# A graph-attention stack whose instruction order is set by the kernel's own list scheduling

## The chip, the cores and the metric

The kernel runs on one core of a Trainium2 chip. A core has TensorE (PE; its weight loads are listed apart as PEld), VectorE (DVE), ScalarE (ACT), GpSimd (POOL) and SyncE (SP); SP and POOL start the transfers here. Each engine works through its own stream of instructions in the order in which they stand, and waits at an instruction until the semaphores that it names are reached. The metric is the device time of the whole kernel in microseconds (us), the median of several runs.

## The reference

The input is x, 32 batches of 512 nodes with 256 features, and one 512 x 512 adjacency matrix that all batches share. Four layers follow each other, each `x = x + layer(relu(layernorm(x)), adj)`:

- Layers 0 and 1 are single-head graph attentions: `Wh = h W`, a score `leaky_relu(s_i + s_j)` for each pair of nodes, where s_i and s_j are products of Wh with two vectors, a softmax over the neighbours, and the weighted mean of Wh, behind which stands an elu (layer 0) or a relu (layer 1).
- Layer 2 is the same with four heads of 64 features.
- Layer 3 is a small network: a linear layer to 512 with relu, an attention over all nodes without a mask (`_gat(relu(out), None, W_fc, a_fc)`), elu and a residual, a linear layer back to 256, a masked attention, elu, a residual and a relu.

All is float32.

## The kernel before

Nodes lie on the 128 partitions in four blocks. A batch's x is one tile of 128 x 4 x 256. Exponentials of scores factor, so that the weights of a pair are `max(r_i, t_j) * mask` and need no exponential of their own: `weights` (line 339) turns the column of r into a row on all partitions by four transposes into a PSUM bank, and DVE makes the four 128 x 512 blocks of w (L353). `aggregate` then multiplies them with the values v on TensorE, and a column of the product is the softmax's denominator, whose reciprocal (L387) scales the result on ACT.

`values` (line 308) makes v: two matmuls into a bank, an exponential of three columns on ACT (L319, L322), in layer 1 a small product on DVE (L324), and a scaled copy of the 256 features on ACT (L320, L325). Layer 2 does it with L462 on ACT and the product L463 on DVE, which reads the bank out. `norm` (L269 to L280) is the layernorm on DVE with two small steps on ACT; `turn_pair` transposes its result and ACT writes it as hT (L290).

The unmasked attention of layer 3 is computed by sorting in all batches but the last (`sort_attend`, line 556): `project_half` (L528, L529 on ACT) makes the values; DVE and ACT count ranks (L586, L599); POOL scatters rows to DRAM in sorted order (L607, eight transfers a batch); SP fetches them as `sums` (L614, L615); DVE builds running sums on each partition (L625 to L632), TensorE carries them over partitions with two matmuls against triangles (`before`, `after`), and DVE adds that (L641, L644); SP writes the result to a table in DRAM (L647, L648). Then POOL gathers one row for each node (L655, four transfers a batch, `g` with two buffers), DVE combines its two halves (L670), and ACT and DVE make elu(elu) of it (L387, L674, L675, L410, L411, L412). `mlp_in` transposes that and adds it to oT (L730).

Four streams (NS = 4) of batches run against each other, 75 model-us apart (LEAD). Each is a generator that yields the time at which it next wants to go on; a loop at the end of `fast` always resumes the stream that is due first. That sets the order in which the program is written down. Each stream has two PSUM banks of its own (8 banks in all) and takes those of idle streams too. The framework's own scheduler then places the instructions on the engines: among those that are ready by its model of durations, the one written first goes first. At five places the kernel ties an instruction to the written order (`keep_in_program_order`): at the minimum of adj (L215) and the first transpose of the mask, at layer 2's weights for j = 0, at the copy T (L625) and at L670.

Of the kernel before, what the change touches and what calls it, by code (L numbers as in the profile page):

```python
# [8 lines left out]

# [1 line left out]

# [11 lines left out]
OP = mybir.AluOpType  # L25
AX = mybir.AxisListType

EPS = 1.0e-5
P = 128
# [2 lines left out]
TINY = 1.0e-30  # L32
CYCLES = 2400.0

@with_exitstack
def fast(ctx, tc, flag, x, adj, w0, a0, w1, a1, w2, a2, mlp1_w, mlp1_b, mlp2_w, mlp2_b,
         w_fc, a_fc, w_hand, a_hand, out):
    nc = tc.nc
    B, N, F = x.shape
# [8 lines left out]
    SLOW = 1.5  # L48
    STRETCH = 2.0

    const = ctx.enter_context(tc.tile_pool(name="const", bufs=1))
    work = ctx.enter_context(tc.tile_pool(name="work", bufs=2))
    psum = ctx.enter_context(tc.tile_pool(name="psum", bufs=1, space=bass.MemoryType.PSUM))
    dram = ctx.enter_context(tc.tile_pool(name="dram", bufs=1, space=bass.MemoryType.DRAM))

    turn = [0]
    begun = [0.0]
# [7 lines left out]
        spent[0] += 4 * max(x.shape[-1], P)  # L65
        nc.tensor.matmul(p, w, x, **flags)  # L66

    def transpose(p, x, i, tied=False):
        spent[0] += 2 * P
        instruction = nc.tensor.transpose(p, x, i)  # L70
        if tied:
            tc.keep_in_program_order(instruction)

    active = set()
    banks = [0]
# [9 lines left out]
    ident = const.tile([P, P], FP, name="ident")  # L85
# [5 lines left out]
    seen = const.tile([P, 5 * B], FP, name="seen")  # L91
# [60 lines left out]
    W0, _ = fetched0 = fetch_w(w0, a0_sb, "W0")  # L152
    adj_sb = work.tile([P, NT, N], I32, tag="w", name="adj", bufs=4)
# [3 lines left out]
    W1, _ = fetched1 = fetch_w(w1, a1, "W1")  # L157
# [6 lines left out]
    for h in range(NH):  # L164
        t, r = divmod(h * D, P)
# [8 lines left out]
    WFC, _ = fetched3 = fetch_w(w_fc, a_fc, "WFC")  # L174
    WM2 = const.tile([P, KH, F], FP, name="WM2")
    nc.sync.dma_start(WM2, mlp2_w.rearrange("(k p) f -> p k f", p=P))
    WHA, _ = fetched4 = fetch_w(w_hand, a_hand, "WHA")
# [8 lines left out]
    C = F + 2  # L186
# [14 lines left out]
    differ = const.tile([P, 2], FP, name="differ")  # L201
# [5 lines left out]
    def setup():  # L207

        own = work.tile([P, NT, N], FP, tag="w", name="own", bufs=4)
        nc.vector.tensor_scalar(own, adj_sb, 0.0, None, op0=OP.is_gt)  # L210
        nc.gpsimd.affine_select(
            out=own, in_=own, pattern=[[P, NT], [-1, N]], base=0, channel_multiplier=1,
            compare_op=OP.not_equal, fill=1.0,
        )
        tc.keep_in_program_order(nc.vector.tensor_reduce(differ[:, 0:1], adj_sb, AX.XY, OP.min))  # L215
        nc.vector.tensor_scalar(differ[:, 0:1], differ[:, 0:1], 0.0, None, op0=OP.is_lt)
        for j in range(NT):
            turn[0] = NS - 1 - j % (NS - 1)
            p = bank()
            for t in range(NT):  # L220
                transpose(p[:, t * P:(t + 1) * P], own[:, t, j * P:(j + 1) * P], ident, j + t == 0)
            nc.scalar.copy(maskT[:, j, :], p)
        turn[0] = NS - 1
        yield
        yield from finish_w(fetched1, 0.01)


        least = small([1], "rden")
        nc.vector.tensor_reduce(least, diag, AX.X, OP.min)
        nc.vector.tensor_scalar(differ[:, 1:2], least, 0.0, None, op0=OP.is_le)  # L230
        nc.vector.tensor_copy(W2[:, :, :, :D], raw2.rearrange("p k (h d) -> p k h d", d=D))
        nc.vector.tensor_scalar_mul(A2v[:, :, 1:2], A2v[:, :, 0:1], -0.8)
        nc.vector.tensor_scalar_mul(A2v[:, :, 2:3], A2v[:, :, 2:3], 0.8)
        for k in range(KF):
            project(W2[:, k, :, D:], lambda k, f: raw2[:, k, f * P:(f + 1) * P], k, A2)
            yield
        yield from finish_w(fetched3, 0.2)

        for tri, sign in ((before, 1), (after, -1)):
            nc.vector.memset(tri, 1.0)  # L240
            nc.gpsimd.affine_select(
                out=tri, in_=tri, pattern=[[sign, P]], base=0, channel_multiplier=-sign,
                compare_op=OP.is_gt, fill=0.0,
            )
        ties = work.tile([P, 2 * N - P], FP, tag="w", name="ties", bufs=4)
        nc.vector.memset(ties, TINY)
        nc.gpsimd.affine_select(
            out=ties, in_=ties, pattern=[[-1, 2 * N - P]], base=N - P, channel_multiplier=1,
            compare_op=OP.is_gt, fill=0.0,
        )  # L250
        nc.vector.tensor_copy(band, ties)
        yield
        yield from finish_w(fetched4, 0.2)
# [89 lines left out]
    def weights(r_col, t_col, masked=True, r=None):  # L343

        landed = r is not None
        if not landed:
            r = bank()
            for t in range(NT):
                transpose(r[:, t * P:(t + 1) * P], r_col(t).to_broadcast([P, P]), ident)
        wt = work.tile([P, NT, N], FP, tag="w", name="w", bufs=4)  # L350
        for j in range(NT):
            if masked:
                w = nc.vector.scalar_tensor_tensor(  # L353
                    wt[:, j, :], r, t_col(j), maskT[:, j, :], op0=OP.max, op1=OP.mult
                )
                if landed and j == 0:
                    tc.keep_in_program_order(w)
            else:
                nc.vector.tensor_scalar(wt[:, j, :], r, t_col(j), None, op0=OP.max)
        return wt  # L360
# [202 lines left out]
    def sort_attend(oT, b):  # L563

        halves, ends = fc_values()
        orders = [dram.tile([N, C], FP, tag=f"order{c}", name=f"order{c}", bufs=2) for c in range(2)]
        at = work.tile([P, 2, NT], U32, tag="at", name="at", bufs=4)
        table = tables[b % 2]
# [9 lines left out]
        p = bank()  # L578
# [25 lines left out]
        for c in range(2):  # L604
# [7 lines left out]
            u = flat[c].rearrange("p (t k) n -> p t k n", k=2)[:, :, 1, :]  # L612
# [6 lines left out]
        for c in range(2):  # L619
            yield sort  # L620
            sums = flat[c].rearrange("p (t k) n -> p t k n", k=2)
            u = sums[:, :, 1, :]

            T = small([NT], "T")
            tc.keep_in_program_order(nc.vector.tensor_copy(T, u[:, :, F + 1]))  # L625
            tot = work.tile([P, C], FP, tag="tot", name="tot", bufs=1)
            nc.vector.tensor_tensor(sums[:, 2, 0, :], u[:, 0, :], u[:, 1, :], op=OP.add)
            nc.vector.tensor_tensor(sums[:, 3, 0, :], sums[:, 2, 0, :], u[:, 2, :], op=OP.add)
            nc.vector.tensor_tensor(tot, sums[:, 3, 0, :], u[:, 3, :], op=OP.add)
            nc.vector.tensor_scalar_mul(u[:, 3, :], u[:, 3, :], T[:, 3:4])  # L630
            for t in (2, 1, 0):
                nc.vector.scalar_tensor_tensor(  # L632
                    u[:, t, :], u[:, t, :], T[:, t:t + 1], u[:, t + 1, :], op0=OP.mult, op1=OP.add
                )
            yield after_us(3)

            pv, pu = bank(), bank()
            matmul(pv[:, :C], before, tot, start=True, stop=True)
            matmul(pu[:, :C], after, u[:, 0, :], start=True, stop=True)
            nc.scalar.copy(sums[:, 0, 0, :], pv[:, :C])  # L640
            nc.vector.tensor_tensor(  # L641
                sums[:, 1:, 0, :], sums[:, 1:, 0, :], pv[:, None, :C].to_broadcast([P, NT - 1, C]), op=OP.add
            )
            nc.vector.tensor_tensor(u, u, pu[:, None, :C].to_broadcast([P, NT, C]), op=OP.add)  # L644
            q = 3 * P // 4
            nc.vector.tensor_tensor(tot[q:, :], tot[q:, :], pv[q:, :C], op=OP.add)  # L646
            nc.sync.dma_start(places[:, :, c, :], flat[c])  # L647
            nc.sync.dma_start(table[N:, c * C:(c + 1) * C], tot[P - 1:, :])  # L648
            sort = after_us(1)
# [13 lines left out]
        landed = after_us(6)  # L663
        for t in range(NT):
            yield landed
            y, q = pair(), pair("q")
            g = gs[t]
            z = g[:, :2 * C]
            tc.keep_in_program_order(
                nc.vector.scalar_tensor_tensor(z, z, ends[:, t, 2:3], g[:, 2 * C:], op0=OP.mult, op1=OP.add)  # L670
            )
            rd = reciprocal(z[:, F:F + 1])
            z = z.rearrange("p (c n) -> p c n", c=2)[:, :, :F]
            nc.scalar.activation(q, z, AF.Exp, scale=rd)  # L674
            nc.scalar.activation(y, z, AF.Relu, scale=rd)  # L675
            elu2_plus1(y, q)
            if t + 2 < NT:
                gather(t + 2)
            got.append(y)
            landed = after_us(3)  # L680
            when.append(after_us(4))
            if t == 0:
                continue
            yield when[t - 1]
            mlp_in(oT, got[t - 1], t - 1)
# [84 lines left out]
    while ready:  # L770
        i = min(ready, key=ready.get)
# [23 lines left out]
    p = bank()  # L795
    transpose(p[:1, :P], bad, ident)
    one = const.tile([1, 1], FP, name="one")
    nc.vector.tensor_reduce(one, p[:1, :P], AX.X, OP.max)
    nc.vector.tensor_scalar(flag, one, 0.5, None, op0=OP.is_gt)


@with_exitstack
# [430 lines left out]
```

## Time and profile before

Three runs gave 2930.02, 2930.80 and 2934.68 us; the median is 2930.8 us. The profiled execution has a span of 2929.6 us from its first to its last instruction; the page gives no other time for it.

| engine | busy us | share of the span | instructions |
|---|---|---|---|
| PE (matmul) | 2858.9 | 98% | 15177 |
| PEld (weight loads) | 2329.5 | 80% | 15177 |
| DVE | 2219.9 | 76% | 5676 |
| ACT | 1536.8 | 52% | 3922 |
| POOL | 502.3 | 17% | 515 |

The DMA engines moved 270.89 MB, 92 GB/s over the span. A float32 matmul is recorded as two passes, a transpose as one, so the 15177 records are some 8850 instructions. "Busy" for PE adds up where any matmul is in flight; a matmul of 257 columns is recorded with 382 ns, while the next one starts 217 ns after it.

How to read what follows: in the order of time, a line has its start in us, its duration in us, the engine, the kernel's line, the operation, what it writes and reads, a shape and how many were merged; in brackets behind it how long the engine stood idle ahead of it and what released it.

### The profile page before, as it was taken

How to read it: one execution, taken by the hardware profiler on the slowest of the kernel's cores; microseconds unless marked ns; L12 is line 12 of the kernel's file. 1: busy time of each engine (PE TensorE's matmuls, PEld its weight loads, DVE VectorE, ACT ScalarE, POOL GpSimd, SP SyncE). 2: the span in 40 equal slices, each digit the busy share in tenths (PEclk: the TensorE clock that was granted, in tenths of full speed). 3: DMA queues.
4: the chain of work that ended last, by engine and by line, in shares of the span. 5: the costliest groups of instructions: out<-in, count | busy, mean ns of one | idle time of the engine just before them, and what ended most of it. 6: DMA issues, size and time to landing. Idle time of an engine off the chain costs nothing.

```text
span 2929.6 us, 43083 instructions
## 1 busy us (share of the span) xinstructions
PE 2858.9 (98%) x15177; PEld 2329.5 (80%) x15177; DVE 2219.9 (76%) x5676; ACT 1536.8 (52%) x3922; POOL 502.3 (17%) x515
## 2 busy tenths in 40 slices
PE   8999999999999999999999999999999999999998
PEld 6777887877888877888877888788887788877876
DVE  4677877778778778778778777787787787777764
ACT  4444455555555555555554556545555555555444
POOL 0011112112122111122021121111221111211220
PEclk9999999999999999999999999999999999999999
DMA  3033223233223333233332233222332322323230
GB/s 94 19 102 102 80 88 116 91 98 95 88 94 106 93 100 98 84 102 96 100 102 80 89 115 93 91 97 91 94 116 80 102 93 88 104 93 96 90 107 30
DMA packets 193182, 270.89 MB, mean 92 GB/s; under 512 B 17024, under 2 KB 156094, under 8 KB 192960
## 3 DMA queue, kind: packets, MB, share of 16 engines
q1 hardware_dynamic: 163200, 169.76, 18.5%
q0 software_dynamic: 29760, 98.30, 10.4%
q8 instruction: 123, 2.02, 0.3%
q14 instruction: 99, 0.81, 0.1%
HBM read 152.62 MB, written 115.39 MB: 91 GB/s over the span
## 4 chain that ended last, share of the span: by engine, by line
PE 82%; DVE 10%; ACT 4%; DMA 3%; issue 1%; SPq 0%; POOL 0%; DVEq 0%; POOLq 0%; ACTq 0%
PE b L66 75%; PE b L70 7%; DVE st L269 2%; DMA g<-table,at 2%; DVE sums L641 1%; DVE xn L280 1%; DVE x L406 1%; DVE y L405 1%; ACT v L325 1%; DVE sums L632 1%; ACT y L505 1%; ACT q L504 1%; DVE w L353 1%; ACT hT L290 1%; DVE tot L646 0%
## 5 line engine op out<-in xcount | busy, mean ns | idle before, releaser
L66 PE MATMUL b<-v,w 128*128 128x65 f32 (+1 forms) x7232 | 1218.0, 321 | 10.6 <-DVE w L353 10.5
L66 PEld LDWEIGHTS b<-v,w 128*128 128x128 f32 x7232 | 1050.0, 191 | 168.7 <-issue 56.1
L66 PE MATMUL b<-WFC,oT 128*128 128x256 f32 (+1 forms) x2048 | 495.2, 380 | 0.0
L66 PEld LDWEIGHTS b<-WFC,oT 128*128 128x128 f32 x2048 | 374.5, 189 | 49.3
L66 PE MATMUL b<-W,hT 128*128 128x259 f32 (+1 forms) x1536 | 388.8, 391 | 22.8 <-DVE v L463 14.1
L353 DVE SCALAR_TENSOR_TENSOR w<-b,v,maskT 128x512 f32<-128x512 f32 x512 | 369.4, 744 | 5.1 <-PE b L70 4.1
L607 POOL DMA_INDIRECT order<-v,at x248 | 277.0, 1117 | 490.7 <-DVE oT L730 152.3
L66 PEld LDWEIGHTS b<-W,hT 128*128 128x128 f32 x1536 | 285.3, 192 | 75.3 <-DVE v L463 17.1
L715 POOL TENSOR_TENSOR x<-x,y 128x512 f32<-128x512 f32 x62 | 87.8, 1416 | 1063.7 <-ACT y L713 950.0
L353 DVE SCALAR_TENSOR_TENSOR w<-spread,v,maskT 128x512 f32<-128x512 f32 x384 | 269.5, 742 | 0.0
L66 PE MATMUL b<-hT,WM 128*128 128x512 f32 x512 | 250.0, 599 | 0.7 <-ACT hT L290 0.7
L66 PE MATMUL b<-oT,WM 128*128 128x512 f32 x512 | 231.2, 594 | 0.0
L655 POOL DMA_INDIRECT g<-table,at x124 | 120.9, 975 | 642.8 <-ACT y L675 292.0
L387 DVE RECIPROCAL rden<-b 128x1 f32<-128x1 f32 (+1 forms) x516 | 77.3, 162 | 184.8 <-PE b L66 183.0
L529 ACT ACTIVATE v<-b,ends 128x256 f32<-128x256 f32 x256 | 118.8, 467 | 177.2 <-PE b L66 172.9
L269 DVE BATCH_NORM_STATS2 st<-x 128x6 f32<-128x256 f32 x512 | 193.3, 409 | 6.4 <-DMA x<-in_x_dram 4.1
L412 DVE TENSOR_TENSOR y<-q,y 128x512 f32<-128x512 f32 (+1 forms) x194 | 132.9, 685 | 82.9 <-ACT q L411 45.0
L339 ACT ACTIVATE oT<-b,bias 128x512 f32<-128x512 f32 x128 | 87.7, 686 | 182.7 <-PE b L66 182.0
L290 ACT ACTIVATE hT<-b 128x512 f32<-128x512 f32 x256 | 146.5, 592 | 70.3 <-PE b L70 70.2
L66 PEld LDWEIGHTS b<-oT,WM 128*128 128x128 f32 x512 | 97.5, 191 | 95.7 <-issue 92.4
L70 PE MATMUL b<-ident,xn 128*128 128x128 f32 x1024 | 147.4, 275 | 6.7 <-DVE xn L280 4.0
L70 PEld LDWEIGHTS b<-ident,xn 128*128 128x128 f32 x1024 | 123.7, 143 | 31.9 <-DVE xn L280 5.2
(143 smaller groups left out, 3748.1 us busy)
## 6 DMA issues: line engine op xcount, KB each, us to landing
table<-sums SPq DMA_DIRECT2D x62, 1032.0 KB
sums<-order SPq DMA_DIRECT2D x62, 516.0 KB
spread<-row SPq DMA_DIRECT2D x96, 256.0 KB
x<-in_x_dram SPq DMA_DIRECT2D x32, 512.0 KB
out_dram<-x SPq DMA_DIRECT2D x62, 256.0 KB
sums<-order SPq DMA_DIRECT2D x62, 129.0 KB
order<-v,at POOLq DMA_INDIRECT x248
g<-table,at POOLq DMA_INDIRECT x124
```

Source lines behind the costliest of these rows:

```text
L66: nc.tensor.matmul(p, w, x, **flags)
L70: instruction = nc.tensor.transpose(p, x, i)
L269: nc.vector.bn_stats(st[:, i, :], xt[:, t0 + i, :])
L290: nc.scalar.activation(hT[:, :, t0 * P:(t0 + 2) * P], p.rearrange("p (k n) -> p k n", k=KF), AF.Relu)
L339: nc.scalar.activation(o[:, f, :], p, AF.Relu, bias=bias[:, f:f + 1])
L353: w = nc.vector.scalar_tensor_tensor(wt[:, j, :], r, t_col(j), maskT[:, j, :], op0=OP.max, op1=OP.mult)
L387: nc.vector.reciprocal(r, den)
L412: nc.vector.tensor_tensor(r, q, r, op=OP.add)
L529: nc.scalar.activation(halves[c][:, t, :F], ps[:, :F], AF.Copy, scale=ends[:, t, 0:1])
L607: nc.gpsimd.indirect_dma_start(out=orders[c], out_offset=bass.IndirectOffsetOnAxis(ap=at[:, 0, t:t + 1], axis=0), in_=halves[c][:, t, :], ...
L655: nc.gpsimd.indirect_dma_start(out=g, out_offset=None, in_=table, in_offset=bass.IndirectOffsetOnAxis(ap=at[:, 1, t:t + 1], axis=0),)
L715: (nc.gpsimd if n == 2 else nc.vector).tensor_tensor(xr, xr, y, op=OP.add)
```

## The change

No instruction of the computation is added, removed or altered. All pools are wrapped so that each tile's pool, tag and number of buffers are noted (`Homes`). When everything has been written down, `arrange` reads the list of instructions, finds an order for each engine, and ties every instruction to the one ahead of it with a dependency that carries no semaphore. The framework's scheduler then has one order left on each engine. The five `keep_in_program_order` ties are gone.

The order is found by list scheduling. `price` gives each instruction two durations, how long it holds its engine and when its result is there, by formulas over engine, operation and size. `jobs_of` finds what must come before what: overlapping reads and writes (`real`), and an order among users of a buffer (`soft`). `in_order` plays the program through: an instruction is offered when its predecessors are done and a buffer is free; each engine takes, of those that are ready at its clock, the one that was written first.

```diff
+HANDOVER = {"PE": 40.0, "DVE": 33.0, "Activation": 33.0, "Pool": 70.0, "SP": 28.0}
+LANDING = {"sums": 4400.0, "spread": 3600.0, "table": 5600.0, "x": 5000.0, "order": 2850.0, "g": 5000.0}
+SWITCH = 93.0
...
+def price(job, outs, ins, in_psum):
+    e, op = job.engine, job.op
+    if op == "Matmult":
...
+        job.passes = 2 if whole and not turned else 1
+        job.load = 109.0 * elements(still) / P * job.span / P
+        job.flow = 109.0 if turned else (elements(moving) * (5.0 / 6.0 if whole else 0.45) + 2.4) * job.span / P
+        return
...
+    if op == "DMACopy":
...
+        job.took = LANDING.get(kind, 2300.0) if large else 2250.0
+        job.holds = 1270.0 if e == "Pool" else 600.0 if kind in ("sums", "table") else 400.0
+        return
+    if e == "DVE":
...
+        elif op in ("TensorTensor", "TensorReduce") or len(wide) > 1:
+            t = 155.0 + 1.042 * n + (55.0 * columns if op == "TensorScalarPtr" else 0.0)
...
+        job.holds = max(45.0, t - 84.0)
+    elif e == "Activation":
...
+            t = 170.0 + 0.82 * n + 90.0 * min(columns, 1)
...
+        job.holds = max(60.0, t - 100.0)
...
+def in_order(jobs, users, homes):
...
+    while placed < len(jobs):
+        for e in order:
+            while coming[e] and coming[e][0][0] <= clock[e]:
+                _, place, job = heapq.heappop(coming[e])
+                heapq.heappush(waiting[e], (place, job))
+        nexts = [(clock[e] if waiting[e] else coming[e][0][0], e) for e in order if waiting[e] or coming[e]]
+        at, e = min(nexts)
+        job = heapq.heappop(waiting[e])[-1] if waiting[e] else heapq.heappop(coming[e])[-1]
+        tags = [slot(n) for n in job.opens if slot(n)]
+        if any(not free[tag] or min(free[tag]) > at for tag in tags):
+            offer(job)
+            continue
...
+        order[e].append(job)
...
+def arrange(tc, homes):
+    jobs, users = jobs_of(list(tc.nc.cur_bb.bb.instructions), homes)
+    edge = mybir.DependencyInfo(mybir.DependencyClass.NoSync, mybir.DependencyReason.DATA)
+    for line in in_order(jobs, users, homes).values():
+        for a, b in zip(line, line[1:]):
+            tc.add_manual_dep(b.ins, a.ins.name, edge, reason="arranged")
...
-    const = ctx.enter_context(tc.tile_pool(name="const", bufs=1))
+    homes = {}
+    const = Homes(ctx.enter_context(tc.tile_pool(name="const", bufs=1)), homes)
...
-        tc.keep_in_program_order(nc.vector.tensor_reduce(differ[:, 0:1], adj_sb, AX.XY, OP.min))
+        nc.vector.tensor_reduce(differ[:, 0:1], adj_sb, AX.XY, OP.min)
...
-                if landed and j == 0:
-                    tc.keep_in_program_order(w)
...
-            tc.keep_in_program_order(nc.vector.tensor_copy(T, u[:, :, F + 1]))
+            nc.vector.tensor_copy(T, u[:, :, F + 1])
...
-            tc.keep_in_program_order(
-                nc.vector.scalar_tensor_tensor(z, z, ends[:, t, 2:3], g[:, 2 * C:], op0=OP.mult, op1=OP.add)
-            )
+            nc.vector.scalar_tensor_tensor(z, z, ends[:, t, 2:3], g[:, 2 * C:], op0=OP.mult, op1=OP.add)
...
     nc.vector.tensor_scalar(flag, one, 0.5, None, op0=OP.is_gt)
+    arrange(tc, homes)
```

## The prediction

> **What bounds the kernel now.** I read the engine shares first, then the chain, the groups by shape, and the order of time around gaps of TensorE.
>
> ```profile
> span 2929.6 us, 43083 instructions
> PE 2858.9 (98%) x15177; PEld 2329.5 (80%) x15177; DVE 2219.9 (76%) x5676; ACT 1536.8 (52%) x3922; POOL 502.3 (17%) x515
> ...
> PEclk9999999999999999999999999999999999999999
> ...
> PE 82%; DVE 10%; ACT 4%; DMA 3%; issue 1%; SPq 0%; POOL 0%; DVEq 0%; POOLq 0%; ACTq 0%
> ```
>
> TensorE bounds the span, its clock is granted throughout (0.996 on average), yet 17% of the chain runs through DVE, ACT and DMA. "98% busy" hides gaps, because matmuls overlap: a record lasts longer than the step to the next. The step itself is read from dense stretches in the order of time of TensorE:
>
> ```profile
> 1214.33 3.60 PE L66 MATMUL b<-oT,WM 128*128 128x512 f32 x8
> 1217.76 1.46 PE L66 MATMUL b<-v,w 128*128 128x257 f32 x6
> ...
> 1222.49 3.68 PE L66 MATMUL b<-v,w 128*128 128x65 f32 x32
> 1226.01 0.61 PE L70 MATMUL b<-ident,xn 128*128 128x128 f32 x4
> 1226.45 1.04 PE L66 MATMUL b<-WHA,rT 128*128 128x259 f32 x4
> ```
>
> Start to start: 8 of 512 columns take 3.43 us, 429 ns each; 32 of 65 columns 3.52 us, 110 each; 4 transposes 0.44 us, 109 each; about 217 for 256 to 259 columns. The trace's median steps (429.5, 111.5, 109, 215.5 to 218, and 226 for 268 columns) times the counts of the groups (1024 of 512, 4096 of 65, some 2500 transposes, 6968 of 256 to 259, 512 of 268, some 70 narrow ones of 0.1) give 2806 us. The first matmul starts at 6.7 us; 8.5 us lie behind the last one's start. So 2929.6 - 2806 - 6.7 - 8.5 = 108 us is all that TensorE loses to gaps, and all that a new order can win. Gaps over 30 ns, counted one by one, sum to 111.7: 35.1 before 190 us, 62.6 up to 2790, 14.0 behind.
>
> The Trainium skill (Perfetto Trace Analysis, Identifying the Most-Contended Engine) judges TensorE's headroom by the share of weight loads instead, here 80%: by it 600 us would be open. The steps above leave 108, because in dense stretches the loads rest too while columns stream; I go by the steps.
>
> What ends the gaps shows in the order of time, at two places that return every 355 us (four batches):
>
> ```profile
> 1894.44 0.76 DVE L670 SCALAR_TENSOR_TENSOR g<-g,ends 128x516 f32<-128x516 f32 x1 [3.77 <-DMA g<-table,at]
> 1895.12 0.87 DVE L463 SCALAR_TENSOR_TENSOR v<-b,rs,v 128x256 f32<-128x256 f32 x2
> ...
> 1895.65 2.95 PE L66 MATMUL b<-W,hT 128*128 128x268 f32 x12 [2.92 <-DVE v L463]
> ```
>
> ```profile
> 1234.30 1.14 PE L66 MATMUL b<-W,hT 128*128 128x259 f32 x4 [0.23 <-ACT v L325]
> ...
> 1678.76 1.03 PE L70 MATMUL b<-ident,xn 128*128 128x128 f32 x8
> 1680.59 0.70 PE L66 MATMUL b<-v,w 128*128 128x257 f32 x2 [0.79 <-DVE w L353]
> ```
>
> In the first, DVE stands at a gathered row that has not landed, layer 2's L463 is queued behind it, and TensorE waits for the bank that L463 frees. In the second, TensorE has come to a group a little too early. Both are faults of order.
>
> **The change, part by part.** No instruction goes or comes, so no busy time changes; only gaps can. In the built programs 5915 of 8847 TensorE instructions keep their place, but 559 of 5554 on DVE, 1526 of 3800 on ACT, 386 of 514 on POOL and 333 of 508 on SP. For each instruction I took the work (at the trace's own steps) that the new order puts ahead of it on its engine less what stood there, and set this against each gap: the waiting matmul's shift later and its releaser's shift earlier both shorten it. A shift earlier helps only if the releaser's own input is there, so the low end counts TensorE's shift alone.
>
> - Waits for ACT's v (L325, L320), middle: 44 gaps, 19.9 us. The matmul gets 0.43 to 0.87 us more work ahead of it, the release comes 0.5 to 0.8 us up in ACT's queue in three of five. TensorE's shift alone wins 15.5, both 19.6. I take 18.
> - Waits for weights (DVE L353), middle: 7 gaps of 0.96, 6.7 us. The matmul goes 0.87 back, but the release 0.65 too: 1.6 won; 6.1 if DVE's added work falls into idle time. I take 1.6.
> - Small ones in the middle (L632, L412, L290, L280): 6.9 us; releasers move up by more than their gaps. Ends 0.7 and 6.8; I take 5.
> - L463, 8 gaps of 0.4 to 3.1 us, 15.7 in all. Of a batch's four gathers, the new order has DVE take the second before the third (before, the third was waited for while the second lay there, 1894.44 against 1899.35) and puts 18 instructions between first and third there. That gives the third's landing (3.8 to 6.8 us from issue, median 4.6) cover. But L463 itself stands 0.8 us of work later, and the fourth gather's product between two L463s. Ends: 7.7 lost, 15.7 won; I take 8.
> - Start (layers' chains of one or two batches): 35.1 us, ends 0 and 18.2 (TensorE's shift alone 9.8); nothing else is there to fill, so I take 9. Tail: 14.0 us, ends 0 and 9.7; I take 5.
> - 236 gaps without any wait, some 0.1 us each, 23.2 us in all (in the three stages): order doesn't touch them; nothing.
> - POOL and SP keep their sequence of work but for neighbours: the fourth gather goes ahead of the next batch's two small copies and eight scatters, and the large loads of both halves of the sums go ahead of their small ones. POOL is 17% busy; the fourth gather is about 1 us that the scatters stand behind. Ends 0 and 31 us if every batch's scatters were late on the path; nothing taken, since scatters begin some 10 us behind that gather now.
>
> Sum of gains: 18 + 1.6 + 5 + 8 + 9 + 5 = 46.6.
>
> New waits stand against it. The last gather's chain (L670, its reciprocal, L674, L675, L411, L410, L412) moves 8 to 16 us of work ahead on DVE and ACT; it takes 0.75 + 0.16 + 0.43 + 0.69 = 2.0 us of DVE and 0.72 + 0.71 + 0.72 = 2.15 us of ACT, and what it passes comes later: L463, L462, L529, L319, L581. By displacement alone 361 of 2335 waits of TensorE in the middle come up short, against none before. Most of that is no loss: between 1885.98 and 1894.44 DVE idled 0.79 + 1.77 + 0.84 + 3.77 = 7.2 us, more than the chain takes. Ends: nothing, and 31 sorted batches times the 3.0 us of the worst gap, 93 us. I take 0.5 us a batch, between the rows of 0.4 (L325) and 0.96 (L353), 16 us.
>
> 46.6 - 16 = 30.6 us. The profiled span is 2929.6, the median of the runs 2930.8, 1.2 us above it; the sum is taken off the median: **2900 us**.
>
> The Trainium skill (Perfetto Trace Analysis, Optimization Strategy) speaks against part of this: a gap that repeats on the saturated engine can mean too few buffers for the next tile. L463 is such a wait for a bank, with two to a stream; if buffers were the cause, the 8 us would not come and the sum would give 2908. The row shows DVE waiting for a transfer ahead of it, so I keep them.
>
> **Rivals.**
> - *Slower: DVE's head is blocked.* All ties are fixed now, so a product of a gathered row placed ahead of its landing stops all of DVE, and L463 or L353 with it. For it: the first product moves 4.3 us of DVE work ahead, where before it had some 2.9 us to spare (in the batch shown: issued at 1875.9, landed 4.9 later, taken at 1883.65). Against it: the order reckons 5.0 us for a landing, above the median, and the chain ahead of the gather moves up by about 1 us too. It decides from 46.6 / 31 = 1.5 us a batch; at 2 us a batch 62 - 46.6 = 15 lost, 2946.
> - *Gaps only change place.* The releasers' shifts give nothing since their inputs set them, and TensorE's shifts alone win 36.6, which new waits of 1.2 us a batch take back: 2931. For it: DVE is idle 24%, so much of its queue is ahead of its inputs anyway.
> - *All of it.* Every gap shrinks by both shifts, L463 goes, nothing new: 76 us, 2855.
> - That the ties don't hold is excluded by the built program: nine in ten DVE instructions stand elsewhere.
>
> **How the numbers follow.** Mine (2880 to 2920) 0.55; near all of it (below 2880) 0.10; a small gain (2920 to 2925) 0.10; gaps change place 0.07; DVE's head blocked 0.18. No change means within 0.2% (5.9 us), about what a measurement of this kernel tells apart: faster 0.75, same 0.07, slower 0.18. The range leaves some 0.1 at each end: 2870, two thirds of the way from 2900 to the best end, to 2942, where the blocked head costs 1.9 us a batch.
>
> **What would show it.** Right: busy times as before; gaps for L325 and L320 in the middle near 2 us in all, L463's below 8; DVE's idle time for gathered rows (26.2 us, 9 times, now) not above 60, each short; start and tail shorter by some 14 us together. Wrong: waits for L463, L529 or L319 in every batch, DVE idle for gathers in most batches, or the first 190 us unchanged.

## The result and the profile after

The changed kernel takes 2956.6 us in the median of four runs (2953.7 to 2959.5), the kernel before 2932.7 us in the four runs beside it: 1.0075 times as long (95% interval 1.0058 to 1.0092), 24 us slower. I had predicted 2900. The direction is that of the rival with DVE's blocked head. The runs below were timed in three further groups, each with the kernel before beside it (medians 2934.6, 2937.1 and 2937.8 us), so "of before" is within a group, and a difference in us to after or between groups can be off by a few us.

In the changed file the lines have moved: L353 of before is L597, L325 is L569, L320 is L564, L463 is L705, L529 is L771, L629 is L871, L632 is L874, L646 to L648 are L888 to L890, L670 is L911, L211 is L455, and TensorE's helpers L66 and L70 are L312 and L316. In the fences they have these new numbers; in e6, e9 and e12 one more, in e4 and e11 two more. The text keeps the numbers of before.

The page of after, shares of the engines and the chain that ended last:

```profile
span 2956.2 us, 43101 instructions
PE 2861.3 (97%) x15177; PEld 2329.9 (79%) x15177; DVE 2233.8 (76%) x5676; ACT 1531.5 (52%) x3922; POOL 508.5 (17%) x515
...
PEclk9999999999999999999999999999999999999999
...
PE 49%; issue 23%; DVE 10%; DMA 10%; ACT 5%; POOL 2%; SPq 0%; POOLq 0%; ACTq 0%; DVEq 0%
```

Work and clock are as before; busy times moved by 14 us at most, on DVE. What changed is the chain: TensorE's part fell from 82% to 49%, transfers rose from 3% to 10%, and "issue" from 1% to 23%. "Issue" is time for which the profile shows no wait; around 1100 us it stands in pieces of some 39 us on POOL. So the shares tell where the chain runs, not what each part costs; the waits say more. First DVE's waits of after (sum in us, times, longest), cut to those for transfers and one ordinary neighbour, then TensorE's:

```profile
DVE g L911 <- DMA g<-table,at: 73.5, 84, 2.6
...
DVE y L647 <- ACT y L747: 48.0, 36, 1.7
...
DVE tot L871 <- DMA table<-tot: 29.2, 15, 2.4
```

```profile
PE b L312 <- DVE tot L871: 20.3, 15, 1.6
PE b L312 <- DVE v L705: 11.9, 17, 2.2
PE b L312 <- DVE w L597: 10.8, 14, 1.0
PE b L316 <- ACT v L569: 7.8, 14, 0.7
PE b L316 <- POOL own L455: 6.8, 1, 6.8
...
PE b L312 <- ACT v L771: 5.6, 13, 1.0
```

DVE stood 9 times at a gathered row before, 26.2 us in all; now 84 times. Its wait at `tot` was not there at all, and it tops TensorE's list.

TensorE's gaps, counted as in the prediction (step from start to start less the form's dense step, gaps over 30 ns), for this kernel and those of the experiments that say most. The dense steps sum to some 2804 to 2807 us in every one. Gaps that show no wait, and some smaller ones, are in the sums but have no row:

| gaps, us | before | after | e1 | e3 | e5 | e13 | e11 | e15 |
|---|---|---|---|---|---|---|---|---|
| first 190 us | 35.1 | 43.3 | 39.4 | 40.6 | 42.3 | 42.2 | 37.5 | 34.7 |
| middle | 62.6 | 86.8 | 59.4 | 61.4 | 32.7 | 27.7 | 77.2 | 102.2 |
| of it: `tot` (L629) | 0.3 | 21.0 | 0 | 23.6 | 0 | 0 | 0 | 0 |
| of it: L463 | 15.7 | 16.3 | 19.6 | 1.8 | 2.3 | 0 | 23.4 | 26.1 |
| of it: L529 | 0 | 8.2 | 7.3 | 0.2 | 0.5 | 0 | 15.8 | 19.0 |
| of it: L325, L320 | 19.9 | 12.6 | 12.6 | 12.5 | 12.6 | 12.6 | 12.6 | 12.6 |
| of it: weights (L353) | 6.7 | 10.5 | 9.3 | 10.5 | 9.3 | 9.3 | 9.3 | 9.3 |
| last 140 us | 14.0 | 9.2 | 10.9 | 8.5 | 9.2 | 7.2 | 12.0 | 12.1 |

From before to after the gaps grew by 27.5 us and the first matmul started 0.9 us earlier: 26.6, which is what the span grew by. Three rows make it: `tot` 20.7, L529 8.2, the start 8.2; L325 and L320 won 7.3 and the tail 4.8.

Two stretches of after in order of time show the two large ones. First `tot`:

```profile
2330.74 0.43 DVE L888 TENSOR_TENSOR tot<-tot,b 32x258 f32<-32x258 f32 x1
2330.77 0.56 SPq L889 DMA_DIRECT2D table<-sums  x1
...
2331.38 0.53 SPq L890 DMA_DIRECT2D table<-tot  x1
2331.39 2.73 DVE L597 SCALAR_TENSOR_TENSOR w<-b,v,maskT 128x512 f32<-128x512 f32 x4
...
2336.18 0.43 DVE L871 TENSOR_TENSOR tot<-sums 128x258 f32<-128x258 f32 x1 [2.00 <-DMA table<-tot]
...
2336.66 0.70 PE L312 MATMUL b<-tot,before 128*128 128x258 f32 x2 [1.39 <-DVE tot L871]
```

SP sends 1 MB of the table, and then 1 KB, the row of `tot`. `tot` has one buffer, so its next write on DVE (L629, for the other half) must wait until that row has left. DVE goes on 4.80 us after the row's issue. By the marks that a transfer sets when it is complete, the row lands 1.1 us after its issue where no megabyte was issued just ahead of it, and 4.5 to 5.1 us where one was; in all 15 such cases its mark comes within 0.4 us of the last of the megabyte's own. In 16 of the 31 sorted batches the order on SP is row, megabyte, row, megabyte; in the other 15 it is megabyte, row, row, megabyte. DVE stands at `tot` in just these 15, and in none of the 16. Before, the first half's row, the one that L629 waits for, went ahead of both megabytes in all 31 batches.

Second, layer 2 behind a gather:

```profile
1107.77 0.76 DVE L911 SCALAR_TENSOR_TENSOR g<-g,ends 128x516 f32<-128x516 f32 x1 [1.19 <-DMA g<-table,at]
...
1111.89 0.76 DVE L911 SCALAR_TENSOR_TENSOR g<-g,ends 128x516 f32<-128x516 f32 x1 [1.96 <-DMA g<-table,at]
...
1114.16 0.48 DVE L705 SCALAR_TENSOR_TENSOR v<-b,rs,v 128x256 f32<-128x256 f32 x1
1114.70 2.45 PE L312 MATMUL b<-W,hT 128*128 128x268 f32 x6 [2.18 <-DVE v L705]
```

Twice within 5 us DVE stands at a row that has not landed, 3.15 us together; L463 comes 2.2 us late to free TensorE's bank. It is the picture from 1894 us of before, now spread over the batches.

### The profile page after: what moved, and what is told of

Same layout as the page of the kernel before. It is cut to its first block, busy times and chain, and to the rows that moved or that the text cites. A ratio compares the mean times of both kernels' runs of the same rounds, so it can differ in the third digit from the quotient of the medians.

```text
span 2956.2 us, 43101 instructions
## 1 busy us (share of the span) xinstructions
PE 2861.3 (97%) x15177; PEld 2329.9 (79%) x15177; DVE 2233.8 (76%) x5676; ACT 1531.5 (52%) x3922; POOL 508.5 (17%) x515
## 4 chain that ended last, share of the span: by engine, by line
PE 49%; issue 23%; DVE 10%; DMA 10%; ACT 5%; POOL 2%; SPq 0%; POOLq 0%; ACTq 0%; DVEq 0%
PE b L312 44%; DMA g<-table,at 7%; PE b L316 5%; DVE w L597 2%; DMA order<-v,at 2%; DMA table<-tot 1%; DVE st L513 1%; DVE g L911 1%; POOL g L897 1%; ACT q L914 1%; POOL order L849 1%; ACT hT L534 1%; ACT y L915 1%; DVE sums L886 1%; POOL x L955 1%
## 5 line engine op out<-in xcount | busy, mean ns | idle before, releaser
L312 PE MATMUL b<-v,w 128*128 128x65 f32 (+1 forms) x7232 | 1212.8, 321 | 11.2 <-DVE w L597 10.8
L312 PEld LDWEIGHTS b<-v,w 128*128 128x128 f32 x7232 | 1054.9, 191 | 187.7 <-issue 82.7
L312 PE MATMUL b<-WFC,oT 128*128 128x256 f32 (+1 forms) x2048 | 492.6, 381 | 6.5 <-ACT v L771 5.6
L312 PEld LDWEIGHTS b<-WFC,oT 128*128 128x128 f32 x2048 | 375.0, 190 | 60.0 <-ACT v L771 9.3
L312 PE MATMUL b<-W,hT 128*128 128x259 f32 (+1 forms) x1536 | 395.3, 391 | 13.9 <-DVE v L705 11.9
L849 POOL DMA_INDIRECT order<-v,at x248 | 284.1, 1145 | 662.7 <-DVE w L597 270.7
L597 DVE SCALAR_TENSOR_TENSOR w<-b,v,maskT 128x512 f32<-128x512 f32 x512 | 363.6, 744 | 5.6 <-PE b L316 5.1
L312 PEld LDWEIGHTS b<-W,hT 128*128 128x128 f32 x1536 | 283.4, 192 | 68.2 <-DVE v L705 23.3
L597 DVE SCALAR_TENSOR_TENSOR w<-spread,v,maskT 128x512 f32<-128x512 f32 x384 | 269.5, 741 | 0.7 <-DMA spread<-row 0.7
L955 POOL TENSOR_TENSOR x<-x,y 128x512 f32<-128x512 f32 x62 | 80.0, 1290 | 1003.9 <-ACT y L953 992.5
L312 PE MATMUL b<-hT,WM 128*128 128x512 f32 x512 | 246.0, 593 | 1.4 <-ACT hT L534 1.4
L629 DVE RECIPROCAL rden<-b 128x1 f32<-128x1 f32 (+1 forms) x516 | 80.0, 162 | 211.4 <-PE b L312 209.9
L312 PE MATMUL b<-oT,WM 128*128 128x512 f32 x512 | 231.5, 595 | 0.0
L771 ACT ACTIVATE v<-b,ends 128x256 f32<-128x256 f32 x256 | 121.2, 474 | 183.9 <-PE b L312 182.0
L663 ACT ACTIVATE q<-b,rden 128x256 f32<-128x256 f32 x128 | 60.4, 472 | 246.9 <-DVE rden L629 246.9
L312 PEld LDWEIGHTS b<-oT,WM 128*128 128x128 f32 x512 | 95.4, 190 | 93.9 <-issue 91.8
L316 PE MATMUL b<-ident,xn 128*128 128x128 f32 x1024 | 149.2, 276 | 6.2 <-DVE xn L524 4.3
L652 DVE TENSOR_SCALAR q<-q 128x512 f32<-128x512 f32 (+1 forms) x194 | 81.9, 422 | 94.3 <-ACT q L914 47.1
```

The lines of the kernel that those rows point to most:

```text
L597: nc.vector.scalar_tensor_tensor(wt[:, j, :], r, t_col(j), maskT[:, j, :], op0=OP.max, op1=OP.mult)
L629: nc.vector.reciprocal(r, den)
L652: nc.vector.tensor_scalar(q, q, 1.0, None, op0=OP.min)
L771: nc.scalar.activation(halves[c][:, t, :F], ps[:, :F], AF.Copy, scale=ends[:, t, 0:1])
L849: nc.gpsimd.indirect_dma_start(out=orders[c], out_offset=bass.IndirectOffsetOnAxis(ap=at[:, 0, t:t + 1], axis=0), in_=halves[c][:, t, :], ...
L955: (nc.gpsimd if n == 2 else nc.vector).tensor_tensor(xr, xr, y, op=OP.add)
```

## The experiments

All of them compute the whole reference; none leaves work out. Each is the changed kernel with the edit shown. The first four ran beside each other and ask which of the two waits costs what, whether the start can be mended by one price, and whether the tied order of one engine is good by itself.

**e1: the row written ahead of the megabyte.** Among what is ready, `in_order` takes what was written first, so the written order of these four lines is the order on DVE and SP.

```diff
-            nc.vector.tensor_tensor(u, u, pu[:, None, :C].to_broadcast([P, NT, C]), op=OP.add)
 ...
-            nc.sync.dma_start(places[:, :, c, :], flat[c])
 ...
+            nc.vector.tensor_tensor(u, u, pu[:, None, :C].to_broadcast([P, NT, C]), op=OP.add)
+            nc.sync.dma_start(places[:, :, c, :], flat[c])
```

> The changed kernel with one thing moved in what is written down: the small sum tot and its one-row transfer to the table stand ahead of the large addition to u and the 1 MB transfer, so that the order found puts the row first on SP in all 31 sorted batches (before this edit the 1 MB went first in 15 of them). Theory A, the row's transfer queued behind the 1 MB makes DVE stop at the next write of tot: the 15 stops of 1.7 to 2.4 us on DVE go, TensorE's gaps for tot fall from 22.8 us to under 2, and the time falls by 18 to 23 us to about 2935. Theory B, a rigid order that lies too close to its inputs, so that a gap taken away opens elsewhere: tot's gaps go but the sum of gaps falls by less than 8 us, time above 2948.

Measured: 2927.8 us, 0.9978 of before (0.9968 to 0.9988), 29 us under after, more than the 18 to 23 expected. DVE's wait for the row and TensorE's for `tot` are gone, and the gathers' is not:

```profile
DVE g L911 <- DMA g<-table,at: 79.6, 91, 4.5
```

The `tot` gaps went (21.0 to 0), some gaps without a wait in the middle with them (4 to 7 us, by how they are told apart), and 3.9 at the start. Little came back elsewhere: L463 took 3.3.

**e2: the load of adj priced by its own landing.** It lands 8.1 us after its issue; `price` gave it 2.3.

```diff
-LANDING = {"sums": 4400.0, "spread": ...
+LANDING = {"adj": 8100.0, "sums": 4400.0, "spread": ...
```

> The changed kernel with one more price: the load of adj is reckoned with 8.1 us, as the trace shows it, and not with 2.3. Theory A: the mask's 16 transposes go behind the first layernorm's again, the gap of 7.15 us at 13.7 us goes, the start's gaps fall from 43 us to about 35, and the time falls by 6 to 10 us to about 2949; nothing changes behind 190 us. Theory B: the start is bound by its chain of loads whatever the order, so that the gap only splits up: less than 3 us.

Measured: 2962.8 us, 1.0095 of before (1.0076 to 1.0114), no better than after. The gap that I blamed on the price went (L211's, 7.15 to 1.24 us), and another took its place at 14.3 us:

```profile
14.30 1.86 PE L312 MATMUL b<-W0a,wT 128*128 128x3 f32 x8 [7.44 <-POOL W0a L355]
```

W0a's second half is issued at 3.98 us and lands at 13.65 in after, where both halves had landed by 3.4 us before. `jobs_of` takes the two loads, whose columns interleave, for an overwrite, and so puts the second behind the first. At the start a price alone only moved the wait to the next load.

**e3: gathers reckoned at 5.8 us instead of 5.0.** From the start of POOL's issue to the last completion mark, the gathers of after take 4.1 to 7.2 us, median 5.0, 95th percentile 6.1, and before much the same. The figures of the prediction and of the texts below (3.8 to 6.8, median 4.6, 95th percentile 5.7) are 0.3 to 0.4 us short of that.

```diff
-... "order": 2850.0, "g": 5000.0}
+... "order": 2850.0, "g": 5800.0}
```

> The changed kernel with the landing of a gathered row reckoned with 5.8 us and not 5.0 (the trace has a median of 4.6 and 5.7 at the 95th of 100). Theory A, DVE stopped at rows that have not landed (73.5 us in 84 waits, 26.2 in 9 before) is what keeps layer 2's release late: DVE's wait for gathered rows falls below 40 us, TensorE's gaps for L463's product from 16.3 to under 9, time 6 to 10 us less, about 2948. Theory C, these waits of DVE lie in time that it has to spare: its waits fall, but TensorE's gaps stay within 3 us, time 2953 to 2960.

Measured: 2934.1 us, 0.9998 of before (0.9988 to 1.0008), 22 us under after: two to three times what I expected. The two waits of DVE in e3:

```profile
DVE g L911 <- DMA g<-table,at: 49.9, 58, 3.4
...
DVE tot L871 <- DMA table<-tot: 31.2, 15, 2.4
```

The gathers' wait fell by a third only, but the gaps behind it nearly all went: L463's 16.3 to 1.8, L529's 8.2 to 0.2. `tot` stayed. So L529's gaps, on ACT, had the same cause, and it is the places where DVE stands, not the sum of its standing, that count. Only 4 of the 58 waits of e3 (5 of 58 in e5) are for a row that took longer than 5.8 us to land. In the others DVE was ready less than 5.8 us after the row's issue (median of all 58 4.6 us), earlier than the plan meant, so the price is a margin for the plan's other errors too, not for the spread of landings alone.

**e4: no ties on DVE.** The other engines keep theirs; DVE is left to the framework's scheduler.

```diff
-    for line in in_order(jobs, users, homes).values():
+    for e, line in in_order(jobs, users, homes).items():
+        if e in ("DVE",):
+            continue
```

> The changed kernel with the ties left out on DVE alone, whose order the framework's scheduler then finds as in the kernel before; PE, ACT, POOL and SP stay tied. Theory A, prices for a few transfers are wrong: SP's order stays, and the stops at tot with it, so the time stays between 2945 and 2965. Theory D, the order of DVE as such costs the time: it falls to 2940 or below. Theory B, orders of several engines that were found apart don't fit: above 2965.

Measured: 3127.0 us, 1.0661 of before (1.0634 to 1.0688), the slowest of all. The largest waits of DVE and of TensorE in e4:

```profile
DVE g L913 <- DMA g<-table,at: 194.3, 118, 4.6
DVE rden L631 <- PE b L314: 133.9, 124, 4.4
DVE T L869 <- DMA sums<-order: 100.9, 51, 5.0
```

```profile
PE b L314 <- ACT v L773: 72.2, 28, 5.2
PE b L314 <- DVE v L707: 22.4, 19, 3.3
```

With the other four engines tied, the tied DVE order is far better than the framework's. That two orders found apart do not fit each other is one reading. Another is not separated from it: the kernel before ties T (L625), L670 and two more places on DVE to the written order, and e4 has none of these ties, so its DVE order is not found "as in the kernel before"; two of its three largest waits stand at just T and L670. The granted clock was 0.977 in e4's profile, against 0.996 before, but the dense steps sum to 2810 us, so that is a few us of the loss.

**e5: both mends, row first and gathers at 5.8.**

> Both edits that helped, in one kernel: the row's transfer written ahead of the 1 MB one, and 5.8 us reckoned for a gathered row. Theory A, two separate wrong prices: their gains add (29 and 22 us), gaps for tot and for L463's product both under 3 us, sum of gaps 85 to 95 us, time 2900 to 2912. Rival, one late place seen twice (DVE's queue late by 2 us at either): the gains overlap, time 2920 to 2928.

Measured: 2901.5 us, 0.9875 of before (0.9858 to 0.9891), 55 us under after, where the two alone gave 29 + 22 = 51. Against the kernel before of each group the steps are 28, 23 and 59 us. So the gains add, or a little more, and they are two faults and not one. The middle is at 32.7 us of gaps, against 62.6 before.

**e6: e5 with the start mended.** adj at 8.1, and two loads that SP issues into one tile no longer counted as an overwrite.

```diff
+                both = write and wrote and job.op == other.op == "DMACopy" and job.engine == other.engine == "SP"
-                if meets and (write or wrote) and other is not job:
+                if meets and (write or wrote) and other is not job and not both:
```

> The kernel with both of these edits, and for the first loads: adj reckoned with 8.1 us, and two loads on SP into one tile no longer counted as one overwriting the other (the two halves of W0a stand in every third column each; taken for overlapping, the second went out at 3.98 us and landed at 13.65, before at 1.3 and 3.4). Theory: 8.1 us for adj alone only laid open the next late input, W0a (a gap of 9.5 us at 14.3 us in that run); with both mended the start's gaps fall from 40 to 28 to 35 us and the time by 5 to 12 us against the kernel with the two edits. Rival, the start is bound by its loads: 3 us or less.

Measured: 2923.6 us, 0.9946 of before (0.9926 to 0.9967), 22 us above e5, a miss. The exception holds for the loads of `sums` too, and that changed the body. DVE's waits in e6:

```profile
DVE T L868 <- DMA sums<-order: 147.2, 61, 6.9
```

In after this wait came to 2.9 us in 4. The plan now sets the copy T 4.3 us behind its load (6.8 in e5), and DVE stands there in 61 of 62 cases: a blocked head again, made by an edit elsewhere in the rules.

**e9: e6 with 190 ns instead of 40 for a result of TensorE to be noticed.** It asks whether the many short gaps come from orders that are too tight by a tenth of a microsecond.

```diff
-HANDOVER = {"PE": 40.0, "DVE": 33.0, ...
+HANDOVER = {"PE": 190.0, "DVE": 33.0, ...
```

> The same kernel with the start mended, and 150 ns more reckoned from a matmul to its reader on another engine (190 for 40). Theory E, the order places things to the nanosecond, so that each small delay on the chip (the 0.1 us gaps without a wait) comes through at the next wait: more room takes 5 us or more out of the gaps for weights and for ACT's v. Theory A, only wrong prices cost: within 5 us of the kernel without it, to either side.

Measured: 2921.6 us, 0.9951 of before (0.9934 to 0.9967), the same as e6. The weights' gaps fell (9.9 to 0.9 us) while those for L325 and L320 rose (20.1 to 28.3): exchanged, not won.

**e11: after, with the row priced at what it takes behind the megabyte.** The written order stays; the plan is only told the truth about the wait.

```diff
+        if kind == "table" and not large:
+            job.took = 5300.0
```

> The changed kernel with the price of the one-row transfer to the table alone corrected, 5.3 us for 2.25; SP still sends the 1 MB first in 15 of 31 batches, but DVE now has 3 to 6 more instructions ahead of the next write of tot. Theory A, it is DVE standing still that costs: its wait for the row falls from 29 us to under 8, TensorE's gaps for tot from 22.8 to under 8, time 2930 to 2942. Rival, the row's lateness costs as such, since tot's product on TensorE is late whatever DVE does meanwhile: the wait goes, the gaps stay above 15, time 2948 or more.

Measured: 2948.3 us, 1.0043 of before (1.0026 to 1.006), 8 us under after, where e1 won 29. DVE's waits in e11:

```profile
DVE g L913 <- DMA g<-table,at: 110.2, 102, 3.2
...
DVE tot L873 <- DMA table<-tot: 1.0, 1, 1.0
```

The time is the rival's, yet TensorE's gaps for `tot` went, as theory A has it, so neither holds whole. The wait at `tot` went as in e1, but the gathers' rose from 73.5 to 110.2 us. It seems that the plan filled the place with gathered products that it believes landed after 5.0 us: L463's gaps rose from 16.3 to 23.4 us and L529's from 8.2 to 15.8. With one price still too short, mending the other mostly moved the loss.

**e12: e5 with the start mended as in e6, but for the constants' tiles alone.**

```diff
+                both = write and wrote and job.op == other.op == "DMACopy" and homes.get(name, ("",))[0] == "const"
```

> The kernel with the two edits that add (row first, 5.8 us for a gathered row), with adj reckoned at 8.1 us, and loads on SP into one tile no longer taken to overwrite each other, but for the weights' and vectors' tiles alone; in the run with the start mended that held for the sums as well, T was then planned 4.3 us behind its load (6.8 before), and DVE stood still for it 147 us in 61 waits. Theory A: with the sums as they were, DVE's wait for sums is back under 10 us, the middle's gaps are back at 30 to 37 us (51 with it), the start is at or below 42, time 2890 to 2903. Rival, the moved start shifts the four streams against each other and so costs in the middle: the middle stays above 45, time above 2912.

Measured: 2903.5 us, 0.9881 of before (0.9859 to 0.9902), the same as e5. The wait at T is back at 3.1 us, so e6 lost by the body and not by the start. The start itself stayed at 43.2 us of gaps: L211's wait fell to 1.7, and the first layernorm's came instead (here L525 is L280 of before):

```profile
PE b L317 <- DVE xn L525: 10.2, 4, 8.0
...
PE b L317 <- DMA W<-in_L_gnn_W_dram: 6.7, 1, 6.7
```

**e13 and e15: how far the reckoned landing matters.** e5 with gathers at 6.8, above all but one of the 124 landings of after, and at 4.2, below the median of 5.0.

```diff
-... "order": 2850.0, "g": 5800.0}
+... "order": 2850.0, "g": 6800.0}
```

> The kernel with the two edits that add, and 6.8 us for a gathered row, the largest landing in the trace. Theory A, a price too high costs little, one too low much: DVE's wait for gathered rows falls below 20 us (51 at 5.8), time within 6 us of 2901. Rival, a late price leaves the product, its chain and the next layer too late: 2910 or more.

> The kernel with the two edits that add, but 4.2 us for a gathered row, below the median of 4.6. Theory A: DVE waits for gathered rows in nearly every batch, 100 us or more in all; gaps for L463's product 20 us or more, time 2925 or more. Rival, 5.0 just happened to fall badly and any other value does better: time below 2912.

Measured: e13 2892.6 us, 0.9844 of before (0.9824 to 0.9864), and e15 2973.9 us, 1.0141 (1.0108 to 1.0173). With e1 and e5, which differ from them in this number alone:

| reckoned landing of a gather, us | 4.2 (e15) | 5.0 (e1) | 5.8 (e5) | 6.8 (e13) |
|---|---|---|---|---|
| time, us | 2973.9 | 2927.8 | 2901.5 | 2892.6 |
| DVE's waits for gathers, us (times) | 128.8 (108) | 79.6 (91) | 51.1 (58) | 4.2 (4) |
| gaps in the middle, L463 and L529, us | 45.1 | 26.9 | 2.8 | 0 |

DVE's wait in e15 and, as a second fence, in e13; then e13's shares of the chain:

```profile
DVE g L911 <- DMA g<-table,at: 128.8, 108, 4.2
```

```profile
DVE g L911 <- DMA g<-table,at: 4.2, 4, 2.4
```

```profile
PE 91%; DVE 5%; ACT 3%; issue 1%; DMA 0%; POOL 0%; SPq 0%; DVEq 0%; ACTq 0%
```

One number in a table of prices, within the measured spread, is worth 81 us, monotonically. The last step, e5 to e13, is small against the groups' noise (0.9858 to 0.9891 and 0.9824 to 0.9864 of before), but the gaps of the profiled runs fall with it, by 7 us. In e15, 16.8 us more of the middle's gaps end with the layernorm's L276, another product of DVE. In e13 transfers are gone from the chain. It beats both kernels: 45 us under before, 64 under after, more than the 6 us under e5 that theory A allowed.

## Why the prediction was wrong

**The bound and the room for a new order: right.** Dense steps sum to about 2806 us in all kernels of the table, the clock stayed at 0.995 to 0.997 there, and what an order can win or lose is in the gaps. The best run took the middle's gaps from 62.6 to 27.7 and the tail's from 14.0 to 7.2, within the 108 us of the prediction. Weight loads by themselves would have promised 600; in e13, 64 us better than after, PEld's share is 81% instead of 79%, so it did not measure the room that an order has.

**"New waits ... I take 0.5 us a batch, 16 us": the term that failed.** Against the 30.6 us forecast the span grew by 26.6, a miss of 57 us. In the sum 13 of them stand in this term and 43 in gains that did not come (below); but the two mends that take away the waits for transfers win 55 us, so those waits are what turned the gain into a loss. `tot` and L529 alone cost 28.9 us, and the gain set down for L463 did not come for the same reason. My ends (0 and 93) held it, but the size came from rows of ACT and weights (0.4 and 0.96), none of which was a wait for a transfer; and I worked through one source, the last gather's chain. I had named the sign myself, DVE "idle for gathers in most batches", and had 60 us as the bound for them: 73.5 came, in 84 waits.

**"POOL and SP keep their sequence of work but for neighbours ... nothing taken": the step behind the largest row.** I had seen the large loads of `sums` go ahead of small ones, but had not gone through the writes to the table in the same list: in 15 batches a 1 KB transfer was set behind 1 MB, and a tile with one buffer hung on it. I looked for late scatters and did not ask who waits for a small transfer to leave. e1 takes away just that: 29 us.

**The argument against the blocked head was the wrong statistic.** "The order reckons 5.0 us for a landing, above the median": by the completion marks 5.0 us is the median itself (56 of the 124 gathers of after take longer), and the prediction's reading of 4.6 was too short. A median also says little here: half of the landings are under it, but where DVE comes to a row that has not landed, DVE stops, and TensorE behind it where no slack is left. The runs at 4.2, 5.0, 5.8 and 6.8 us show that a price near the upper end is needed: the step from 5.0 to 5.8 won 26 us, that to 6.8 some 9 more. Part of that is margin for a plan that is off elsewhere, as the waits of e3 show. The rival gave 2946 at 2 us a batch. Its mechanism came, but it held one of the two faults; I gave it 0.18.

**Gains, one by one.** Of 46.6 us:
- L325 and L320: 18 taken, 7.3 came. The profile sign "near 2 us" was wrong, 12.6 remained, and remained in nearly every kernel, so neither fault holds it. A gap of after shows what still ends it:

```profile
2331.20 0.16 DVE L568 TENSOR_TENSOR both<-rs,v 128x1 f32<-128x1 f32 x1
...
2331.39 0.48 ACT L569 ACTIVATE v<-b,both 128x256 f32<-128x256 f32 x1 [0.46 <-DVE both L568]
...
2331.92 0.65 PE L316 MATMUL b<-ident,v 128*128 128x128 f32 x4 [0.42 <-ACT v L569]
```

  ACT is free and waits for a one-column product of DVE. A displacement on ACT's queue and on TensorE's says nothing of that third engine; I had set such a bound for ACT's shift, yet taken 18 by both. Before, ACT waited for this product (L324) in all 36 gaps of the middle that L325 ends. In after it does so in 14 of 21, 5.9 of their 11.9 us; in the other 7 ACT comes from other work without a pause.
- Weights: 1.6 taken, 3.8 lost. Neither mend brought it back (9.3 in e5 and e13); what moved it was e9's dearer handover, against L325. Small ones in the middle: 5 taken; L632 won 1.7 and L412 2.2.
- L463: 8 taken, 0.6 lost. With landings reckoned at 6.8 us all 15.7 came. So the cover that I described is a real one where the plan believes in late landings; at 5.0 it placed the products too early. The Trainium skill (Perfetto Trace Analysis, Optimization Strategy) says that such a repeated gap can mean too few buffers for the next tile; the number of banks is the same in after, with 16.3 us, and in e13, with none. For these gaps the price decided, not the buffers. At `tot`, one buffer is part of the fault; a second one was not tried, and the order alone removed the wait.
- Start: 9 taken, 8.2 lost. I had bounded it by "0 and 18.2" and so excluded a loss without a reason. adj's price and W0a's second half account for waits there (e2, e12), but mending both left 43.2 us. What bounds the start stays open; that waits exchange places there among the loads is all that the runs show. Tail: 5 taken, 4.8 came.

**What was right by size, with the wrong kernel.** Net 30.6 us was expected. With the two faults mended the same scheduling gives 36 us (e5) and 45 us (e13) under the kernel before. That is in part luck: in e5 the start still loses 7.2 us instead of winning 9 and L325 with L320 wins 7.3 instead of 18, while L463 wins 13.4 instead of 8, gaps without a wait shrink that I had put at nothing, and most of the 16 us of new waits stays away. The room was rightly judged; that this order used it was not.

## What to carry to other kernels

Where one engine's fixed order contains waits for transfers, reckon each transfer at the upper end of its measured landings, which also leaves the plan some margin, and judge a reordering by the spread, not the median. Go through the order on the transfer queues as through that on an engine: for each small transfer ask what large one it now stands behind, and which single-buffered tile hangs on it. After mending one such price look at the others again, since a plan fills the room with whatever it still prices too low (e11, e6).

## What the runs showed that I had not expected

- A 1 KB transfer lands 1.1 us after its issue when it is first, and 4.5 to 5.1 us after it right behind a 1 MB one on the same queue: the price of a transfer is that of its place. The Trainium skill (DMA: Bandwidth & Descriptors, Queues, rings and completion order) has a rule that bears on it: a transfer's completion is signalled only after every earlier write of the same DMA engine. The 4.5 to 5.1 us agree with it, and so do the row's marks within 0.4 us of the megabyte's last; which step of the transfer takes the time, no run here shows.
- The loss behind a blocked head is far from proportional to the blocking. From 79.6 to 51.1 us of DVE's waits for gathers (e1 to e5) the time fell by 26 us; from 51.1 to 4.2 (e5 to e13) by some 9.
- Untying one engine of five, the ties of the kernel before left out too, cost 170 us against after, more than all gaps of TensorE in the kernel before (111.7).
- Some 23 us of TensorE's gaps before, 0.1 us each, show no wait at all (26 us in after; 32 and 34 if every gap counts in which no semaphore came). The order that leaves fewest gaps, e13, has 5.4 us of these in the middle against 12.0 before (6.4 against 16.2), so they are not fixed as I had assumed; what makes them is open.
